# A graph layer with experts on one core: the order check's list and the x rows for u loaded behind z, u begun with the first edge tile

## The chip, the cores and the metric

The kernel runs on one core of a Trainium2 chip. Times are microseconds of device time of one execution, and smaller is better. The core has five engines with a queue of instructions each: TensorE (PE, with its weight loads shown as PEld), VectorE (DVE), ScalarE (ACT), GpSimd (POOL) and SyncE (SP). An engine takes its queue in order and waits on semaphores that other engines and transfers raise. SP, ACT and POOL also issue the transfers (DMA).

## What is computed

`x` has 6250 rows of 256 numbers, and there are 100000 edges `src -> dst`, sorted by `dst`. A graph layer is followed by a layer of 8 experts of which each row uses two:

```python
h = layernorm(x)
msg_sum = segment_sum(h[src], dst);  deg = segment_sum(1, dst)
agg = msg_sum / maximum(deg, 1)
x = x + concat([h, agg]) @ W.T + b                     # W: 256 x 512
n = layernorm(layernorm(x)) * gamma + beta
w = softmax of the top 2 of (n @ Wr + br)              # 8 experts
x = x + sum_e w[e] * (gelu(n @ W1[e] + b1[e]) @ W2[e] + b2[e])
```

## The kernel before, in words

The product with W is split in two. Its right half is applied to every row before the edges are summed: `z = layernorm(x) @ W_right.T`, with eight more columns that hold the router's logits. Its left half gives `u = x + layernorm(x) @ W_left.T + b`, with the same eight columns. Both are written to memory as `z_d` and `u_d`. Then `x1 = u + (sum of z over a row's edges) / deg`.

**The z stage** (`z_block`, line 278) runs over 13 blocks of four 128-row tiles, the last block being one tile. For each tile TensorE forms `product(t, 1)` (line 260, two products of depth 128, into the tiles `ph` and `pm` in turn), ScalarE scales it by `rstd_x` into `zt` (284), and SP writes `z_d` (287). VectorE takes the statistics of x some tiles ahead (`ahead`, lines 184 and 185) and makes `rstd_x` of eight tiles at a time (173 to 179). After each pair of tiles from block 5 on, one piece of other work is taken from the list `steps`: constants, the placing of the windows, the check that `dst` is sorted (`check_order`, 310 and 311, which compares `dst` with the same list moved by one, `follow`), and the sum of all checks (`sum_wrongs`, 366). SP loads x and its transpose four blocks ahead; behind the first four blocks stand the loads of `dst_i`, `src_i`, `follow` (302 to 304) and `gb_sb`.

**Between z and the edges** the left half of W is made ready: its router columns (`router_columns(0)`, 226 and 228), the biases spread over lanes (233 and 234), the columns' mean taken off (`center_weights(0)`, 248 to 253), and the biases' products (`add_biases`, 241 to 243). 28 tiles `xg` that will hold gathered rows get a column of ones (485).

**The edge stage.** The edges are cut into 56 windows of 14 tiles of 128 edges, 784 edge tiles in all. For an edge tile POOL gathers 128 rows of `z_d` by `src_i` into one of the 28 `xg` tiles (`gather`, 566), VectorE has made a matrix of zeros and ones from `dst` (`hot_tiles`, 574 and 577, seven edge tiles at a time), and TensorE adds the product of the two to the window's sum `pS` (`add_edges`, 583, two passes). A gather for tile t + 28 may start once the edge tile t has been added. The loop over edge tiles is a list of ticks: at each tick one edge tile is added, one gather is issued, and functions that `at(tick, f)` put down for later are called. When a window ends, its sum is shared with the next window through memory (589, 593, 597, 605), `u_d` is fetched (610) and x1 is formed (623 to 625). Each four windows go through the routing (493 to 537, 541 to 551, 631 to 663), the sorting of rows (670, 673) and, from 60 ticks after their end, the experts (849, 854, 862, 866), whose instructions TensorE's queue holds between the edge tiles.

**The u stage** has no place of its own. `u_stages()` issues the x loads of three pairs of tiles and returns 26 steps. A step loads x for a pair three steps on (197), adds the bias row (376), forms two products (260) and adds them in (383, 384), and writes the pair before to `u_d` (388). Before the first edge tile six steps are taken; then one step at every second tick, so that the last comes at tick 38. Then the memory of the u stage is handed to the experts: `xe` is cleared in four parts (828, ticks 3, 8, 13 and 18 later) and 16 loads bring the experts' weights (971, every second tick).

All five engines are under a schedule written by hand: each engine's queue holds the instructions in the order in which the program names them.

Of the kernel before, what the change touches and what calls it, by code (L numbers as in the profile page):

```python
# [8 lines left out]
F32 = mybir.dt.float32  # L9
I32 = mybir.dt.int32  # L10
# [7 lines left out]
P = 128  # L18
EPS = 1e-5
C = 14  # L20
# [7 lines left out]
XG = 28  # L28
# [2 lines left out]
@with_exitstack  # L31
def gnn_ffn_kernel(ctx: ExitStack, tc: tile.TileContext, x, x_cols, src, dst, dst_next, gw, gw_t, gb, gb_cols, gamma, beta,
                   wr, br, w1, b1, w2, b2, out):

# [32 lines left out]
    nc = tc.nc  # L67
# [6 lines left out]
    W = src.shape[1]  # L74
    DZ = D + NX
    DA = DZ + 1
# [22 lines left out]
    const = ctx.enter_context(tc.tile_pool(name="const", bufs=1))  # L99
# [25 lines left out]
    edges = fast_pools.enter_context(tc.tile_pool(name="edges", bufs=1))  # L125
    rstd_x = edges.tile([P, NT], F32, name="rstd_x")
    u_pools = fast_pools.enter_context(ExitStack())
    u_pool = u_pools.enter_context(tc.tile_pool(name="u", bufs=2))
# [3 lines left out]
    early = early_pools.enter_context(tc.tile_pool(name="early", bufs=2, side="right"))  # L132
# [25 lines left out]
    lanei = early.tile([P, 1], I32, name="lanei", bufs=1)  # L158
    nc.gpsimd.iota(lanei, pattern=[[1, 1]], base=0, channel_multiplier=1)

    def constants():
        nc.vector.tensor_scalar(before, ej, 0.0, None, op0=ALU.is_lt)
        nc.scalar.activation(cols, coli, AF.Copy)
        nc.vector.tensor_copy(lane, lanei)
        nc.vector.tensor_scalar(upper, col, lane, None, op0=ALU.is_gt)
# [79 lines left out]
    def center_weights(h):  # L245
        pc = ps.tile([P, DZ], F32, name="pm")
        for k in range(KD):
            nc.tensor.matmul(pc, ones, gw_sb[:, h * KD + k, :], start=(k == 0), stop=(k == KD - 1))
        for k in range(KD):
            nc.vector.scalar_tensor_tensor(gc[:, h * KD + k, :DZ], pc, -1.0 / D, gw_sb[:, h * KD + k, :],  # L250
                                           op0=ALU.mult, op1=ALU.add)
            if h == 0:
                nc.vector.tensor_copy(gc[:, k, DZ:], rc[:, k, :])
# [36 lines left out]
            if between:  # L290
                between.pop(0)()

    src_i = const.tile([P, W, C], I32, name="src_i")
    dst_i = const.tile([P, W, C], I32, name="dst_i")
    wrong = const.tile([P, 3], F32, name="wrong")

    def load_edges():

        follow = early.tile([P, W, C], I32, name="follow", bufs=1)
        nc.sync.dma_start(dst_i, dst)
        nc.sync.dma_start(src_i, src)
        nc.sync.dma_start(follow, dst_next)
        return follow

    def check_order(follow, i):
        some = slice(i * W // 2, (i + 1) * W // 2)
        down = early.tile([P, W // 2, C], F32, name="down", bufs=1)
        nc.vector.tensor_tensor(down, dst_i[:, some], follow[:, some], op=ALU.is_gt)  # L310
        nc.vector.reduce_max(wrong[:, i:i + 1], down.rearrange("p g c -> p (g c)"), axis=AX.X)

# [56 lines left out]
    def u_stages():  # L369

        def load(B):
            B.x = load_x(u_pool, "xu", B.first, B.n, UB, 4)

        def one(B):
            B.ut = u_pool.tile([P, UB, DZ], F32, name="u_t", bufs=3)
            nc.vector.tensor_tensor(B.ut[:, :B.n, :D], B.x[:, :B.n, :],
                                    gb_sb[:, None, :].to_broadcast([P, B.n, D]), op=ALU.add)

        def two(B):
            for i in range(B.n):  # L380
                t = B.first + i
                pu = product(t, 0)
                nc.vector.tensor_tensor(B.ut[:, i, D:], pu[:, DZ:], gb_r, op=ALU.add)
                nc.vector.scalar_tensor_tensor(B.ut[:, i, :], pu[:, :DZ], rstd_x[:, t:t + 1], B.ut[:, i, :],  # L384
                                               op0=ALU.mult, op1=ALU.add)

        def put(B):
            nc.sync.dma_start(rows_of(u_d, B.first, B.n), B.ut[:, :B.n, :])

        pairs = []  # L390
        for t0 in range(0, NT, UB):
            B = Group()
            B.first, B.n = t0, min(UB, NT - t0)
            pairs.append(B)

        for B in pairs[:3]:
            load(B)
# [19 lines left out]

    for t0 in blocks[:4]:
        load_block(t0)
    follow = load_edges()  # L420
    gb_sb = u_pool.tile([P, D], F32, name="gb_sb", bufs=1)
    nc.sync.dma_start(gb_sb, bass.AP(tensor=gb.tensor, offset=gb.offset, ap=[[0, P], [1, D]]))
    placed_rows = []
    steps = [constants, lambda: placed_rows.append(place_windows()), lambda: check_order(follow, 0),
             lambda: spread_windows(placed_rows[0]), lambda: check_order(follow, 1), place_rows, check_windows,
             lambda: None, sum_wrongs]
    router_weights()
    router_columns(1)
    center_weights(1)
    ahead, t0 = [], 0  # L430
# [12 lines left out]
    for t0 in blocks:  # L443
        if t0 + 4 * TB in blocks:
            load_block(t0 + 4 * TB)
        elif t0 == blocks[-3]:
            u_tasks = u_stages()
        z_block(t0, steps if t0 >= blocks[5] else None)
    assert not ahead
    assert not steps  # L450
    router_columns(0)
    wide_b = router_biases()
    center_weights(0)
    add_biases(wide_b)
    zero = u_pool.tile([CAP, D], F32, name="zero", bufs=1)
    nc.vector.memset(zero, 0.0)
    early_pools.close()
# [15 lines left out]
    def weights(pool):  # L473
# [5 lines left out]
        for e in range(0, NX, 2):  # L479
            parts += first[e + 2:e + 4] + second[e:e + 2]  # L480
        return w1_sb, w2_sb, parts

    xg = [edges.tile([P, DA], F32, name=f"xg{i}") for i in range(XG)]
    for g in xg:
        nc.vector.memset(g[:, DZ:], 1.0)


    def variances(G):
# [80 lines left out]

    def hot_tiles(V, c):  # L570

# [398 lines left out]
    def at(t, f, *args):  # L970
        later.setdefault(max(t, now), []).append(lambda: f(*args))
# [85 lines left out]
    def new_window(g, V_before):  # L1057
        V = Group()
        V.g, V.before, V.hot = g, V_before, []
        hot_tiles(V, 0)  # L1060
        return V

    V = new_window(0, None)
    edge_tiles = [(g, c) for g in range(W) for c in range(C)]
    for g, c in edge_tiles[:XG]:
        gather(g, c)
    for _ in range(6):
        u_tasks.pop(0)()
    for index in range(W // CW):
        K = Group()  # L1070
        K.index, K.first = index, index * CW
# [193 lines left out]
```

## Time and profile before

| | |
|---|---|
| median of 5 runs | 1445.03 us (1436.97 to 1447.31) |
| profiled execution | 1435.43 us, its span 1433.6 us |
| busy in the span | PE 1106.7, POOL 844.2, DVE 698.4, ACT 452.9 us |
| mean granted clock of TensorE | 0.886 of full speed |
| last z_d write issued, first gather | 64.35 and 67.78 us |
| first edge tile on TensorE | 79.84 us |
| last u product on TensorE | 161.26 us |

Engine names with a q at the end (SPq, POOLq) are what that engine's queue issues. In a line of the timeline the columns are start, duration, engine, line of the kernel, operation, tiles written and read, shape, count, and in brackets the idle time of the engine before it and what ended that. An edge tile is two records of line 583, a u or z product four records of line 260 (each product is two matmuls of two passes). The profiled execution lies 9.6 us below the median of the runs.

### The profile page before, as it was taken

How to read it: one execution, taken by the hardware profiler on the slowest of the kernel's cores; microseconds unless marked ns; L12 is line 12 of the kernel's file. 1: busy time of each engine (PE TensorE's matmuls, PEld its weight loads, DVE VectorE, ACT ScalarE, POOL GpSimd, SP SyncE). 2: the span in 40 equal slices, each digit the busy share in tenths (PEclk: the TensorE clock that was granted, in tenths of full speed). 3: DMA queues.
4: the chain of work that ended last, by engine and by line, in shares of the span. 5: the costliest groups of instructions: out<-in, count | busy, mean ns of one | idle time of the engine just before them, and what ended most of it. 6: DMA issues, size and time to landing. Idle time of an engine off the chain costs nothing.

```text
span 1433.6 us, 19064 instructions
## 1 busy us (share of the span) xinstructions
PE 1106.7 (77%) x5236; PEld 908.4 (63%) x5236; DVE 698.4 (49%) x2426; ACT 452.9 (32%) x1264; POOL 844.2 (59%) x892
## 2 busy tenths in 40 slices
PE   7858736696987969788786969798798887967752
PEld 6737524575866757576675758567687765855641
DVE  5736745362544545355453625465452544565323
ACT  2300002332342433334242324434323433435210
POOL 0076666666656666666566666666666666554552
PEclk9979978798987979999898989999999998988866
DMA  9878894545445454545445454554545454565543
GB/s 340 308 230 255 258 311 118 114 125 126 126 123 124 123 122 128 130 114 138 119 128 114 133 128 120 122 137 120 129 125 135 121 132 118 139 177 150 151 145 119
DMA packets 151610, 217.67 MB, mean 152 GB/s; under 512 B 37587, under 2 KB 119158, under 8 KB 151370
## 3 DMA queue, kind: packets, MB, share of 16 engines
q0 software_dynamic: 42768, 118.97, 33.3%
q1 hardware_dynamic: 100394, 87.97, 19.3%
q10 hardware_dynamic: 8336, 9.45, 2.0%
q8 instruction: 44, 0.72, 0.2%
q14 instruction: 68, 0.56, 0.1%
HBM read 163.97 MB, written 52.32 MB: 151 GB/s over the span
## 4 chain that ended last, share of the span: by engine, by line
PE 51%; issue 17%; DVE 10%; ACT 7%; another core or an unknown queue 6%; DMA 4%; ACTq 2%; SPq 2%; POOL 1%; POOLq 0%; DVEq 0%
PE pS L583 18%; PE ph L849 14%; PE py L862 10%; PE pm L670 4%; ACT xe L824 3%; PE py L910 2%; PE ph L892 2%; ACT hid L854 1%; ACTq L813 1%; DVE hot L577 1%; PE ph L260 1%; DMA xg<-y_d,plans 1%; PE pm L260 1%; DMA u_d<-u_t 1%
## 5 line engine op out<-in xcount | busy, mean ns | idle before, releaser
L566 POOL DMA_INDIRECT xg<-z_d,src_i x784 | 747.1, 953 | 476.7 <-issue 178.2
L583 PE MATMUL pS<-xg,hot 128*128 128x265 f32 x1568 | 446.6, 418 | 68.1 <-issue 55.6
L583 PEld LDWEIGHTS pS<-xg,hot 128*128 128x128 f32 x1568 | 312.6, 207 | 138.2 <-issue 72.9
L849 PE MATMUL ph<-xe,w_sb 128*128 128x128 f32 x1792 | 268.7, 298 | 94.9 <-issue 87.3
L849 PEld LDWEIGHTS ph<-xe,w_sb 128*128 128x128 f32 x1792 | 250.3, 210 | 118.9 <-issue 100.8
L862 PE MATMUL py<-w_sb,hid 128*128 128x256 f32 x896 | 229.1, 398 | 43.3 <-issue 19.6
L862 PEld LDWEIGHTS py<-w_sb,hid 128*128 128x128 f32 x896 | 176.3, 200 | 83.0 <-issue 48.4
L854 ACT ACTIVATE hid<-ph,b_sb 128x128 f32<-128x128 f32 x448 | 126.3, 375 | 295.4 <-remote 157.6
L824 ACT ACTIVATE xe<-xs x448 | 139.5, 311 | 90.6 <-issue 47.8
L577 DVE TENSOR_TENSOR hot<-cols,rel 128x896 f32<-128x896 f32 x112 | 121.2, 1082 | 87.1 <-PE pS L583 53.0
L941 POOL DMA_INDIRECT xg<-y_d,plans x98 | 95.0, 969 | 100.7 <-DMA out_dram<-xg 41.2
L866 DVE TENSOR_TENSOR rows<-py,b_sb 128x512 f32<-128x512 f32 x56 | 38.3, 685 | 155.0 <-PE py L862 37.7
L589 DVE TENSOR_TENSOR pS<-pS,row 1x265 f32<-1x265 f32 x55 | 23.5, 426 | 183.3 <-PE pS L583 84.9
L593 ACT ACTIVATE sums<-pS 128x265 f32<-128x265 f32 x56 | 22.0, 392 | 251.0 <-issue 101.5
L673 ACT ACTIVATE xs<-pm,beta_sb,gamma_sb 128x256 f32<-128x256 f32 x112 | 57.3, 568 | 135.6 <-PE pS L583 57.1
L260 PE MATMUL ph<-gc,x_t 128*128 128x264 f32 (+1 forms) x200 | 58.6, 418 | 19.8 <-remote 9.0
L670 PE MATMUL pm<-to,xn 128*128 128x256 f32 x224 | 59.9, 387 | 14.1 <-DVE to L663 4.2
L625 DVE SCALAR_TENSOR_TENSOR x<-pS,rdeg,x 128x264 f32<-128x264 f32 x55 | 27.1, 493 | 72.8 <-DMA x<-u_d 48.7
L260 PE MATMUL pm<-gc,x_t 128*128 128x264 f32 (+1 forms) x192 | 55.3, 413 | 8.4 <-DVE u_t L384 6.3
L260 PEld LDWEIGHTS ph<-gc,x_t 128*128 128x128 f32 x200 | 38.6, 201 | 32.5 <-remote 10.5
L670 PEld LDWEIGHTS pm<-to,xn 128*128 128x128 f32 x224 | 41.2, 190 | 26.5 <-issue 8.3
L948 DVE SCALAR_TENSOR_TENSOR xg<-xg,plans,xg 128x256 f32<-128x256 f32 (+1 forms) x98 | 46.0, 483 | 23.9 <-DMA xg<-y_d,plans 15.2
(196 smaller groups left out, 821.0 us busy)
## 6 DMA issues: line engine op xcount, KB each, us to landing
y_d<-rows SPq DMA_DIRECT2D x56, 256.0 KB
xg<-z_d,src_i POOLq DMA_INDIRECT x784
w_sb<-w_dram ACTq DMA_DIRECT2D x16, 512.0 KB
sums_d<-sums SPq DMA_DIRECT2D x55, 132.5 KB
x<-u_d SPq DMA_DIRECT2D x55, 132.0 KB
x_d<-x SPq DMA_DIRECT2D x55, 128.0 KB
u_d<-u_t SPq DMA_DIRECT2D x24, 264.0 KB
x_t<-x_cols_dram SPq DMA_DIRECT2D x12, 512.0 KB
```

What stands on the lines that cost most here:

```text
L260: nc.tensor.matmul(pz, x_t[:, t, k, :], gc[:, h * KD + k, :n], start=(k == 0), stop=(k == KD - 1))
L566: nc.gpsimd.indirect_dma_start(out=xg[(g * C + c) % XG][:, :DZ], out_offset=None, in_=z_d[:, :], in_offset=bass.IndirectOffsetOnAxis(ap=sr ...
L577: nc.vector.tensor_tensor(hot, col[:, None, :].to_broadcast([P, HC, P]), V.rel[:, c:c + HC, None].to_broadcast([P, HC, P]), op=ALU.is_equal)
L583: nc.tensor.matmul(V.pS, V.hot[c // HC][:, c % HC, :], xg[(V.g * C + c) % XG], start=(c == 0), stop=(c == C - 1))
L670: nc.tensor.matmul(px[:, k, :], G.xn[i][:, k * P:(k + 1) * P], G.one_hot[i], start=True, stop=True)
L673: nc.scalar.activation(xs[:, at:at + 2 * P], px[:, k, :], AF.Identity, bias=beta_sb[:, k:k + 1], scale=gamma_sb[:, k:k + 1])
L824: nc.scalar.activation(xe[:, :, bass.ds(to_at, CAP)], src[:, :, bass.ds(src_at, CAP)], AF.Copy)
L849: nc.tensor.matmul(ph[:, i, a * SH:(a + 1) * SH], w1_sb[:, U.e + a, k, c * P:(c + 1) * P], xe[:, k, at:at + SH], start=(k == 0), stop=(k = ...
L854: nc.scalar.activation(U.hid[:, c, a * SH:(a + 1) * SH], ph[:, i, a * SH:(a + 1) * SH], AF.Gelu, bias=b1_sb[:, U.e + a, c:c + 1])
L862: nc.tensor.matmul(U.py[:, h, :], U.hid[:, c, h * P:(h + 1) * P], w2_sb[:, U.e + h, c, :], start=(c == 0), stop=(c == KH - 1))
L941: nc.gpsimd.indirect_dma_start(out=V.y2[r], out_offset=None, in_=y_d[:K.batch.end_row, :], in_offset=bass.IndirectOffsetOnAxis(ap=plans[:c ...
L948: nc.vector.scalar_tensor_tensor(V.o, V.y2[r], plans.bitcast(F32)[:count, n, 2 + r:3 + r], V.o, op0=ALU.mult, op1=ALU.add)
```

## The change

- `follow` is no longer loaded behind the first four blocks but behind the whole of z and behind the first three x loads of u; its tile and that of `check_order` move into the memory of u. `check_order` and `sum_wrongs` leave the list `steps` and are called at the ticks 6, 12 and 18 of the edge loop.
- The first three x loads of u, which were issued ahead of the last three blocks of z, are issued behind z.
- `router_columns(0)`, `router_biases()`, `center_weights(0)` and `add_biases()` become pieces of `steps`, between the products of z.
- The ones of the 28 `xg` tiles are written in the piece `constants`.
- The six u steps before the first edge tile are gone. The 26 steps come at the even ticks 0 to 50.

```diff
     def constants():
+        for g in xg:
+            nc.vector.memset(g[:, DZ:], 1.0)
...
     def load_edges():
-        follow = early.tile([P, W, C], I32, name="follow", bufs=1)
         nc.sync.dma_start(dst_i, dst)
         nc.sync.dma_start(src_i, src)
+    def load_follow():
+        follow = u_pool.tile([P, W, C], I32, name="follow", bufs=1)
         nc.sync.dma_start(follow, dst_next)
         return follow
...
-    steps = [constants, lambda: placed_rows.append(place_windows()), lambda: check_order(follow, 0),
-             lambda: spread_windows(placed_rows[0]), lambda: check_order(follow, 1), place_rows, check_windows,
-             lambda: None, sum_wrongs]
+    steps = [constants, lambda: placed_rows.append(place_windows()), lambda: router_columns(0),
+             lambda: spread_windows(placed_rows[0]), lambda: wide_b.append(router_biases()),
+             lambda: center_weights(0), place_rows, lambda: add_biases(wide_b[0]), check_windows]
...
     for t0 in blocks:
         if t0 + 4 * TB in blocks:
             load_block(t0 + 4 * TB)
-        elif t0 == blocks[-3]:
-            u_tasks = u_stages()
         z_block(t0, steps if t0 >= blocks[5] else None)
-    router_columns(0)
-    wide_b = router_biases()
-    center_weights(0)
-    add_biases(wide_b)
+    u_tasks = u_stages()
+    follow = load_follow()
...
-    xg = [edges.tile([P, DA], F32, name=f"xg{i}") for i in range(XG)]
-    for g in xg:
-        nc.vector.memset(g[:, DZ:], 1.0)
...
     for g, c in edge_tiles[:XG]:
         gather(g, c)
-    for _ in range(6):
-        u_tasks.pop(0)()
+    at(6, check_order, follow, 0)
+    at(12, check_order, follow, 1)
+    at(18, sum_wrongs)
```

More of the change, by code (lines that the diff above doesn't have):

```diff
@@ L159, in gnn_ffn_kernel @@
     nc.gpsimd.iota(lanei, pattern=[[1, 1]], base=0, channel_multiplier=1)
+    src_i = const.tile([P, W, C], I32, name="src_i")
+    dst_i = const.tile([P, W, C], I32, name="dst_i")
+    xg = [edges.tile([P, DA], F32, name=f"xg{i}") for i in range(XG)]
     def constants():
+        for g in xg:
+            nc.vector.memset(g[:, DZ:], 1.0)
         nc.vector.tensor_scalar(before, ej, 0.0, None, op0=ALU.is_lt)
@@ L291, in z_block @@
                 between.pop(0)()
-    src_i = const.tile([P, W, C], I32, name="src_i")
-    dst_i = const.tile([P, W, C], I32, name="dst_i")
     wrong = const.tile([P, 3], F32, name="wrong")
     def load_edges():
-        follow = early.tile([P, W, C], I32, name="follow", bufs=1)
         nc.sync.dma_start(dst_i, dst)
         nc.sync.dma_start(src_i, src)
+    def load_follow():
+        follow = u_pool.tile([P, W, C], I32, name="follow", bufs=1)
         nc.sync.dma_start(follow, dst_next)
@@ L308, in check_order @@
         some = slice(i * W // 2, (i + 1) * W // 2)
-        down = early.tile([P, W // 2, C], F32, name="down", bufs=1)
+        down = u_pool.tile([P, W // 2, C], F32, name="down", bufs=1)
         nc.vector.tensor_tensor(down, dst_i[:, some], follow[:, some], op=ALU.is_gt)
@@ L419, in gnn_ffn_kernel @@
         load_block(t0)
-    follow = load_edges()
+    load_edges()
     gb_sb = u_pool.tile([P, D], F32, name="gb_sb", bufs=1)
@@ L423, in gnn_ffn_kernel @@
     placed_rows = []
-    steps = [constants, lambda: placed_rows.append(place_windows()), lambda: check_order(follow, 0),
-             lambda: spread_windows(placed_rows[0]), lambda: check_order(follow, 1), place_rows, check_windows,
-             lambda: None, sum_wrongs]
+    wide_b = []
+    steps = [constants, lambda: placed_rows.append(place_windows()), lambda: router_columns(0),
+             lambda: spread_windows(placed_rows[0]), lambda: wide_b.append(router_biases()),
+             lambda: center_weights(0), place_rows, lambda: add_biases(wide_b[0]), check_windows]
     router_weights()
@@ L1061, in new_window @@
         return V
+    now = 0
     V = new_window(0, None)
```

## The prediction

> **What bounds the kernel now.** I read the table of stages first, then the chain of waits, then the timeline of the first edge tiles. The table (engines' busy time, granted clock, DMA share, GB/s in each stretch):
>
> ```profile
> 11.00:63.40 52.40, 47.31 (x200) 38.52 (x201) 38.85 (x177) 22.25 (x57) 0.00 (x0) 1.00 1.04 365
> 63.40:67.80 4.40, 4.04 (x27) 3.66 (x26) 2.25 (x38) 0.48 (x1) 0.02 (x1) 1.00 0.62 199
> 67.80:79.60 11.80, 10.25 (x44) 7.79 (x43) 9.89 (x38) 0.00 (x0) 9.06 (x10) 1.00 0.75 227
> 79.60:109.00 29.40, 13.58 (x36) 8.66 (x35) 6.26 (x16) 0.00 (x0) 19.48 (x21) 0.62 0.67 207
> 109.00:162.10 53.10, 46.48 (x190) 37.06 (x189) 36.07 (x97) 0.79 (x2) 35.03 (x35) 0.95 0.86 262
> 180.60:215.50 34.90, 10.15 (x37) 7.46 (x36) 16.28 (x43) 2.50 (x5) 22.69 (x24) 0.72 0.89 303
> 256.00:1433.00 1177.00, 930.92 (x4555) 771.26 (x4553) 551.33 (x1898) 411.85 (x1159) 716.86 (x754) 0.89 0.49 129
> ```
>
> The columns are PE, PEld, DVE, ACT, POOL. From 256 us TensorE carries the kernel, and the change touches nothing there: what is won or lost before comes out at the end one for one. The z stage moves 365 GB/s with its DMA engines full. The odd row is 79.6 to 109: PE, DVE and DMA are all half idle, while POOL issues gathers one behind the other. The timeline shows what stands still:
>
> ```profile
> 86.25 0.17 DVE L383 TENSOR_TENSOR u_t<-ph,gb_r 128x8 f32<-128x8 f32 x1 [3.66 <-remote]
> 87.09 2.15 PE L260 MATMUL ph<-gc,x_t 128*128 128x272 f32 x4 [2.90 <-remote]
> ...
> 98.93 0.17 DVE L383 TENSOR_TENSOR u_t<-ph,gb_r 128x8 f32<-128x8 f32 x1 [6.14 <-remote]
> ...
> 103.92 0.95 POOL L566 DMA_INDIRECT xg<-z_d,src_i  x1 [0.30 <-issue]
> 106.63 0.17 DVE L383 TENSOR_TENSOR u_t<-pm,gb_r 128x8 f32<-128x8 f32 x1 [7.01 <-issue]
> ...
> 107.47 2.15 PE L260 MATMUL pm<-gc,x_t 128*128 128x272 f32 x4 [5.55 <-DVE u_t L384]
> ...
> 109.00 0.94 POOL L566 DMA_INDIRECT xg<-z_d,src_i  x1 [4.13 <-remote]
> ```
>
> Line 383 waits for u products whose matmuls the trace shows long done (the one read at 98.93 began at 80.29). TensorE's results reach the others one at a time: those of products 9, 10, 11, 12 and 13 at 81.30, 86.25, 90.50, 98.93 and 106.63, 6.3 us apart. POOL has run without a break since 67.78; its last free tile is filled by the gather at 103.92, and 2.7 us behind that all is normal. The same is seen far from here, in the experts (764 us on: POOL resumes after a pause, eight gathers later TensorE crawls, and recovers when POOL has to wait again):
>
> ```profile
> 764.12 0.94 POOL L566 DMA_INDIRECT xg<-z_d,src_i  x1 [2.60 <-remote]
> ...
> 772.65 0.27 PE L849 MATMUL ph<-xe,w_sb 128*128 128x128 f32 x1 [0.37 <-issue]
> ...
> 774.08 0.27 PE L849 MATMUL ph<-xe,w_sb 128*128 128x128 f32 x1 [1.16 <-issue]
> ...
> 775.48 0.27 PE L849 MATMUL ph<-xe,w_sb 128*128 128x128 f32 x1 [1.13 <-issue]
> ...
> 778.67 0.94 POOL L566 DMA_INDIRECT xg<-z_d,src_i  x1 [2.37 <-remote]
> ```
>
> So I take it that an unbroken run of some eight gathers slows TensorE until POOL pauses. That is inferred from coincidence, not shown.
>
> **The change part by part.** The sum is against the profiled execution, 1435.43 us (span 1433.6); the median of the runs is 9.6 higher, and I carry the difference over to it.
>
> *z stage.* TensorE gains the pieces that stood at 63.4 to 66.7: router columns 0.95, centring 1.13, biases 0.51 + 0.59, and loses 0.19 of `sum_wrongs`: +3.0 us. Its idle time there is 52.4 - 47.3 = 5.1 us, 1.76 of it at 49.7 behind the `rstd_x` of tiles 32 to 39, so between none and all of the 3.0 is hidden. VectorE gains 0.40 (28 ones), 0.17, 0.28 + 0.29, 2 x 0.43 + 2 x 0.16, 0.16 + 0.16 = 2.64 and loses 2 x (0.53 + 0.56) + 0.12 = 2.30: +0.34. The loads moved out are 0.40 MB (`follow`) and 0.79 MB (three pairs of x); at 365 GB/s 1.1 and 2.2 us. Ends: -3.3 to +3.0. I take 0, near their middle: where z ends, TensorE runs without a gap at 0.89 us a product, which lets neither end through whole.
>
> *Start of the gathers.* The first, at 67.78, waits for the last z write (issued 64.35). That write remains, so 67.8 stays, plus what z gives. The ones of `xg` on VectorE ended at 67.75; they move, and as the gather writes other columns I take the write for what it awaited. SP has three x loads and `follow` (0.4 to 0.7 us each to issue, 2.7 in all) between the last z write and the load of u's first tick; u's first x lands 2.67 behind its issue (the row at 65.11), about 68, before it is read. Cost 0; if POOL's start slips with z, everything slips with it.
>
> *TensorE between z and the first edge tile.* Before, products 0 to 9 of u (0.91 us each) ran from 66.7 to 77.2 under the first gathers. Now the first edge tile stands ahead of them and needs its gather: a gather lands 3 to 4 us behind its issue (3.45 and 3.68 in the chain), so TensorE idles from about 65 to 70.8. That cover is gone, and the ten products come later: 9.1 us of TensorE.
>
> *The slow stretch.* From 70.8 a pair of one edge tile (0.45) and one product (0.91) takes 1.36 us, so five pairs are done by 77.5, where the slow stretch began in this trace, ten gathers into the run. In it a pair takes the 6.3 us of above. POOL now stops when gather 28 + (edge tiles done) has no tile: 67.8 + 1.25 x (28 + 5 + (t - 77.5)/6.3) = t gives 117, with 11 pairs done, and 2.7 us later, at 120, the stretch is over. Before, it was over at 107 to 109 with 17 products done.
>
> *The rest of u.* Product 17 began at 107.47 and product 48 at 161.26: 1.735 us for one product and one edge tile. Products 12 to 48: 37 x 1.735 = 64.2, so u is through at 184 instead of 162.2. Then seven edge tiles instead of nineteen are left of the first four windows, at the 0.95 of that stretch (18.0 us for 19): 190.9 against 180.2. **+10.7 us.** Ends: with the stretch over at 109 and nine products done, 109 + 39 x 1.735 + 6.6 = 183.3, +3; with the POOL run one slot cycle longer (126), +17.
>
> *VectorE in u.* `check_order` at ticks 6 and 12 (1.09 each) and `sum_wrongs` (0.12) add 2.3 us; behind them on VectorE stand `hot` and line 376, and TensorE awaits those. Their list lands before tick 6, so they wait for nothing. Between 0 and 2.3; I take 0, since VectorE is busy 36.07 of 53.1 us in the stretch that such ticks resemble (109 to 162.1).
>
> *Ticks 38 to 50.* The clears of `xe` (2.17 each) move 12 ticks; of the four, the last two now fall among the routing of the first four windows, which TensorE awaits at 215.5. 0 to +4.3; I take 0, as two clears stood in that chain before and were followed by waits on transfers (5.35 us at 187.84). The weights (16 loads) shift likewise; they are needed at tick 116.
>
> Sum: 0 + 10.7 = 10.7; 1435.4 + 10.7 = 1446.1 profiled, **1455.7** against the median; I say 1455.
>
> One rule speaks against the change too. The row: the granted clock was 0.62 in 79.6 to 109, and a product took 2.15 us at 87.09 instead of 1.08. The Trainium skill, "TensorE: Matmul & The Clock Gate", Part 1, says that an idle window of some 3.4 us halves TensorE's clock and that as much activity restores it. By it the idle from 65 to 70.8 would put the first 3.4 us of edge tiles at half speed, an estimate of 1.7 us more; the sum above leaves that out.
>
> **The rivals.**
> - *A, faster: the slow stretch does not come.* It stood between products that ran ahead and 28 gathers; if it is not POOL's run that makes it, or if pauses below eight gathers break it, u runs at 1.735 from the start: 70.8 + 49 x 1.735 + 6.6 = 162.4 against 180.2, -17.8, **1427**. For it: between 110 and 118 POOL issued seven gathers in a row without harm. Against it: the first 28 gathers have free tiles in either kernel. It decides if POOL's first unbroken run ends before some 12 gathers.
> - *B, no change: the loss is taken up behind u.* In 180.6 to 215.5 TensorE is busy 10.15 of 34.9 us. If what it awaits there hangs on transfers and not on the end of the fourth window, 10 us vanish: **1445**, 4 either way. Against it: the routing starts from that window's x1.
> - *C: the z stage gets longer,* by up to the 3.0 of TensorE's pieces, +3 behind whichever of the others holds; it is in the range.
>
> **How the numbers follow.** The slow stretch recurring, 0.52 (1448 to 1462 with its own ends); A 0.28; B 0.20. Half a per cent is 7.2 us, about what a measurement of this kernel can tell from no change. Of the forecast four fifths are beyond 7.2 (0.42), the rest within; nearly all of A is faster (0.26); of B three fifths lie within, a fifth on each side. Slower 0.46, same 0.26, faster 0.28. The range takes in A's centre and the upper end of the slow stretch with z's 3.0 and the clears' 4.3: 1427 to 1466.
>
> **What the profile after would show.** Right: first gather near 67.8; first edge tile near 71, with TensorE idle before it; a stretch from about 78 in which line 383 waits for products long done, ending where POOL first waits for a tile, near 117; the last u product near 183; the fourth window's end near 191. Wrong: no such stretch with POOL still unbroken (then my cause is wrong, and A holds); or the stretch, but the first experts no later than before (B); or the last z write later than 66 (C).

## The result, and the profile after

The changed kernel takes 1443.93 us (median of 36 runs, 1432.58 to 1451.14), the kernel before 1441.95 (62 runs, 1432.56 to 1450.82). The ratio is 1.0012, with a 95% interval of 0.9999 to 1.0024: +1.7 us, between -0.1 and +3.5. The forecast of 1455 us is not what happened, and its case B, "no change", is where the time came out. The profiled execution of the changed kernel took 1446.93 us, its span 1445.1.

The engines' busy time by stage, in the stretches in which the prediction showed them (columns PE, PEld, DVE, ACT, POOL, the granted clock, the share of the DMA, GB/s), kernel after:

```profile
11.00:63.40 52.40, 49.17 (x208) 40.94 (x209) 38.81 (x210) 21.74 (x55) 0.00 (x0) 0.97 0.98 343
63.40:67.80 4.40, 2.43 (x11) 1.72 (x10) 0.00 (x0) 1.71 (x4) 0.00 (x0) 1.00 0.50 171
67.80:79.60 11.80, 3.88 (x9) 3.01 (x10) 3.91 (x19) 0.00 (x0) 8.06 (x9) 0.62 0.95 322
79.60:109.00 29.40, 12.42 (x47) 9.32 (x45) 4.30 (x12) 0.00 (x0) 22.40 (x24) 0.73 0.54 152
109.00:162.10 53.10, 43.43 (x168) 33.38 (x169) 34.90 (x93) 0.79 (x2) 31.80 (x33) 0.88 0.78 225
180.60:215.50 34.90, 17.14 (x56) 12.75 (x56) 23.33 (x48) 2.50 (x5) 24.88 (x27) 0.78 0.94 306
256.00:1433.00 1177.00, 932.25 (x4558) 778.92 (x4558) 552.03 (x1897) 413.32 (x1166) 717.38 (x757) 0.88 0.50 129
```

From 67.8 to 79.6 TensorE has lost its cover (3.88 us busy instead of 10.25), as forecast. From 79.6 to 109 it is as slow as before (12.42 instead of 13.58). From 180.6 to 215.5 it does 7 us more than before (17.14 instead of 10.15): the last u product and edge tiles of the first windows, which before stood earlier, now fall there. The next lines are the timeline of the start and of the slow stretch, kernel after:

```profile
75.72 1.22 PE L580 MATMUL pS<-xg,hot 128*128 128x265 f32 x2 [9.90 <-DMA xg<-z_d,src_i]
76.74 2.02 PE L267 MATMUL ph<-gc,x_t 128*128 128x272 f32 x4
...
81.52 1.08 PE L267 MATMUL ph<-gc,x_t 128*128 128x272 f32 x4
...
84.25 1.08 PE L267 MATMUL ph<-gc,x_t 128*128 128x272 f32 x4
...
86.10 0.17 DVE L387 TENSOR_TENSOR u_t<-pm,gb_r 128x8 f32<-128x8 f32 x1 [2.77 <-issue]
...
98.69 0.17 DVE L387 TENSOR_TENSOR u_t<-ph,gb_r 128x8 f32<-128x8 f32 x1 [11.30 <-remote]
...
108.49 0.17 DVE L387 TENSOR_TENSOR u_t<-pm,gb_r 128x8 f32<-128x8 f32 x1 [9.11 <-remote]
...
109.75 0.94 POOL L563 DMA_INDIRECT xg<-z_d,src_i  x1 [0.30 <-issue]
115.02 0.94 POOL L563 DMA_INDIRECT xg<-z_d,src_i  x1 [4.33 <-remote]
...
116.95 0.17 DVE L387 TENSOR_TENSOR u_t<-ph,gb_r 128x8 f32<-128x8 f32 x1 [7.17 <-remote]
...
118.16 0.56 DVE L314 TENSOR_TENSOR down<-dst_i,follow 128x392 f32<-128x392 int32 x1
```

The slow stretch came back, with the same features: the reads of u products wait 7 to 11 us for products that TensorE had begun long before (the one read at 98.69 began at 84.25), and it is over at 117, just behind POOL's first longer pause (idle for 4.33 us up to the gather at 115.02). The prediction had POOL stop at 117 and the stretch over at 120.

A few moments of single profiles on chips where the kernel before takes some 1440 to 1455 us, in us. A window's end is the end of its last edge tile on TensorE (the prediction's 180.2 for the fourth is 179.7 so read); "sorting" is the first product that sorts rows for experts (line 670 of the kernel before). A third value of before is from the kernel that holds TensorE in window 30 (below), which is the same up to there.

| moment | before | after |
|---|---|---|
| last scaling of z | 63.8, 64.3, 64.5 | 65.9 |
| first gather | 67.8, 68.9, 68.5 | 69.1 |
| first edge tile | 79.8, 79.7, 79.2 | 75.7 |
| last u product's end | 162.3, 163.5, 163.1 | 181.7 |
| fourth window's end | 179.7, 179.9, 179.4 | 184.9 |
| first sorting | 222.1, 224.4, 224.2 | 228.0 |
| 224th edge tile | 426.2, 427.8, 424.8 | 428.6 |
| 784th edge tile | 1255.7, 1259.5 | 1259.4 |
| span | 1433.6, 1442.0 | 1445.1 |

u ends 19 us later, the fourth window 5, the last edge tile 0 to 4. The two spans of the unchanged kernel differ by 8.4 us, half of it behind the last edge tile (177.9 and 182.5 us): a single pair of spans says nothing of a change of this size.

### The profile page after: what moved, and what is told of

Read it like the earlier page. It is cut to its first block, busy times and chain, and to the rows that moved or that the text cites. A ratio compares the mean times of both kernels' runs of the same rounds, so it can differ in the third digit from the quotient of the medians.

```text
span 1445.1 us, 19054 instructions
## 1 busy us (share of the span) xinstructions
PE 1107.7 (77%) x5236; PEld 916.9 (63%) x5236; DVE 698.0 (48%) x2426; ACT 452.8 (31%) x1264; POOL 843.7 (58%) x892
## 4 chain that ended last, share of the span: by engine, by line
PE 56%; issue 18%; DVE 9%; ACT 5%; DMA 4%; another core or an unknown queue 4%; SPq 2%; ACTq 1%; POOL 1%; POOLq 0%; DVEq 0%
PE pS L580 19%; PE ph L846 16%; PE py L859 11%; PE pm L667 3%; ACT xe L821 2%; PE ph L889 2%; PE py L907 2%; DMA u_d<-u_t 1%; DVE hot L574 1%; PE ph L267 1%; ACT hid L851 1%; ACTq L810 1%; PE pm L267 1%; DVE st L191 1%
## 5 line engine op out<-in xcount | busy, mean ns | idle before, releaser
L580 PEld LDWEIGHTS pS<-xg,hot 128*128 128x128 f32 x1568 | 312.0, 206 | 141.2 <-issue 80.4
L846 PE MATMUL ph<-xe,w_sb 128*128 128x128 f32 x1792 | 272.1, 302 | 112.9 <-issue 94.4
L846 PEld LDWEIGHTS ph<-xe,w_sb 128*128 128x128 f32 x1792 | 254.0, 214 | 138.8 <-issue 110.7
L851 ACT ACT_TABLE_LOAD x24 | 30.8, 1283 | 71.5 <-PE pS L580 54.7
```

The costliest lines, as they stand in the source:

```text
L580: nc.tensor.matmul(V.pS, V.hot[c // HC][:, c % HC, :], xg[(V.g * C + c) % XG], start=(c == 0), stop=(c == C - 1))
L846: nc.tensor.matmul(ph[:, i, a * SH:(a + 1) * SH], w1_sb[:, U.e + a, k, c * P:(c + 1) * P], xe[:, k, at:at + SH], start=(k == 0), stop=(k = ...
L851: nc.scalar.activation(U.hid[:, c, a * SH:(a + 1) * SH], ph[:, i, a * SH:(a + 1) * SH], AF.Gelu, bias=b1_sb[:, U.e + a, c:c + 1])
```

## Experiments

The study fell on chips of two kinds: on three the kernel before took medians of 1441.75, 1454.94 and 1443.66 us, on two 1209.81 and 1211.66. Each chip was used on one occasion, so what belongs to the chip and what to the occasion is not told apart. Each comparison of times below is with runs of before on the same chip; the moments of profiles are mostly compared across chips.

### The kernel before once more

No edit; for a second profile.

> The kernel before once more, unchanged, for a second profile of it. It tells how far two profiles of one kernel differ at the same places. If single profiles are good to about 1 us up to the fourth window's end (179.7 us) and to the first sorting (222.1), then the +5.2 and +5.9 us that the changed kernel's profile shows there are the change's. If they scatter by 5 us or more, those readings are worth nothing. The tail behind the last edge tile (177.9 us in the profile of before, 185.7 in that of after) is expected to scatter by several us.

Its profile is in the table: up to the fourth window the two agree to 0.5 us except for the start of the gathers and the end of u (1.1 each), at the first sorting they differ by 2.3. So the 5 us at the fourth window are the change's; of the later ones half could be chance.

### u begun with the first edge tile, alone; and the rest of the change, alone

```diff
-    for _ in range(6):
-        u_tasks.pop(0)()
```

> The kernel before with the six u steps ahead of the first edge tile left out, so that u begins with the first edge tile; nothing else is changed. The theory of the prediction (u late by 22 us, the fourth window late by 10.7, and that carried to the end): about +8 to +11 us. Rival 1 (the fourth window is late by only some 3 us, since edge tiles get ahead in the slow stretch when no u products stand before them, and that is carried to the end): +2 to +4. Rival 2 (the loss is taken up behind u): between -1 and +1, with the fourth window's end still late in the profile.

0.9993 (0.9975 to 1.0011), -1.0 us, with the fourth window's end at 185.1 and the first sorting at 226.4. The other way round, in the kernel after:

```diff
+    for _ in range(6):
+        u_tasks.pop(0)()
     at(6, check_order, follow, 0)
```

> The changed kernel with the six u steps put back ahead of the first edge tile; the rest of the change stays. The theory of the prediction: 8 to 11 us less than the changed kernel, so 6 to 9 less than before. Rival 1: 2 to 4 us less than the changed kernel, the z stage's 2 us remaining. Rival 2: as the changed kernel within 1 us.

1.0008 (0.9989 to 1.0027), +1.2 us; the fourth window ends at 184.0, the first sorting is at 226.5. So, against the mean of 179.7 in before, u's late start by itself costs 5.4 us at the fourth window, the rest of the change, with its late z (last scaling at 68.3 in this profile, first gather at 71.5), 4.3, and both together 5.2: in these single profiles they do not add. At the end none of the three is told from before. The theory of the prediction, 8 to 11 us, is out; with the time unchanged and the fourth window late, the first kernel does what its Rival 2 said.

Where the lateness of u goes is seen on TensorE behind u. First the kernel before, then the kernel after (line 583 of before and 580 of after are the edge tiles):

```profile
162.18 2.40 PE L583 MATMUL pS<-xg,hot 128*128 128x265 f32 x10
167.17 3.37 PE L583 MATMUL pS<-xg,hot 128*128 128x265 f32 x14 [2.59 <-issue]
174.57 5.08 PE L583 MATMUL pS<-xg,hot 128*128 128x265 f32 x14 [4.04 <-issue]
```

```profile
179.04 1.06 PE L580 MATMUL pS<-xg,hot 128*128 128x265 f32 x4
180.57 1.16 PE L267 MATMUL ph<-gc,x_t 128*128 128x272 f32 x4 [0.47 <-issue]
181.56 3.29 PE L580 MATMUL pS<-xg,hot 128*128 128x265 f32 x14
186.93 0.46 PE L580 MATMUL pS<-xg,hot 128*128 128x265 f32 x1 [2.08 <-issue]
```

With u done, the kernel before adds edge tiles in lots of seven and waits 2.59 and 4.04 us in between. In the kernel after there are u products at that time, which fill these waits, and the last tiles of the window then run at 0.45 us each without one.

### A hold on TensorE of known length

The first edge tile of window 3 (the fourth) or of window 30 is formed 44 times more, and overwritten:

```diff
     def add_edges(V, c):
...
+        for _ in range(44 if V.g == 3 and c == 0 else 0):
+            nc.tensor.matmul(V.pS, V.hot[0][:, 0, :], xg[V.g * C % XG], start=True, stop=True)
...
```

> The kernel before with TensorE held for about 20 us at the first edge tile of the fourth window: that tile's product is formed 44 times more (about 0.45 us each) and overwritten. The theory of the prediction (what the fourth window loses comes out at the end one for one): the fourth window ends near 200 instead of 180, the first sorting near 242 instead of 222, and the time is 20 us longer. Theory that the loss is taken up behind u: the fourth window near 200, the sorting between 222 and 242, the 224th edge tile (426 to 428) less than 5 us later, and the time less than 5 us longer.

> The same hold of about 20 us on TensorE, but at the first edge tile of window 31, in the middle of the experts. If TensorE's work bounds the time from 256 us on, as the prediction said, about +20 us. If POOL's gathers bound it, less than +10, since 28 gathered tiles (some 35 us of POOL's work) are ready ahead. It tells whether a loss at this place is carried where one at the fourth window is not.

The holds and what stands behind the first, kernel with the hold in the fourth window:

```profile
168.22 21.58 PE L584 MATMUL pS<-xg,hot 128*128 128x265 f32 x88 [3.94 <-issue]
189.64 12.67 PE L585 MATMUL pS<-xg,hot 128*128 128x265 f32 x56
...
239.90 1.10 PE L672 MATMUL pm<-to,xn 128*128 128x256 f32 x4 [3.68 <-DVE to L665]
```

21.6 us held; the fourth window ends at 196.1, the first sorting is at 239.9 and the 224th edge tile at 441.3. Against the profile of the same chip (the third values of the table) that is +17, +16 and +17: some 5 us of the hold were taken up within the fourth window, whose tiles then run without a wait (second line). The time is 1.0139 (1.0119 to 1.0158), +20 us with 17 to 23. In window 30, 19.8 us held are 1.0131 (1.0089 to 1.0174), +19 with 13 to 25. So a loss of this size at the fourth window is carried to the end: for it that sentence of the prediction holds, and the routing behind it, rival B's place, takes up no more than 1 us. That a loss of 5 us is carried too does not follow. A hold stops POOL at once, and the late u does not: the 71st gather is at 190.5 with the hold, at 173.2 in the kernel after and at 170.0 and 171.5 in before. But at the 106th gather the kernel after is 4.3 us behind the mean of these two profiles of before, so POOL does fall behind there too, only later.

### Fewer gathered tiles for the first four windows

```diff
+RING, RT = 8, 56
...
+    def slot(t):
+        return t % RING if t < RT else t % XG
...
-            out=xg[(g * C + c) % XG][:, :DZ], out_offset=None, in_=z_d[:, :],
+            out=xg[slot(g * C + c)][:, :DZ], out_offset=None, in_=z_d[:, :],
...
```

The loop over the edge tiles, not shown, issues the gathers as these tiles come free, at most two at a tick.

> The kernel before with the first 56 edge tiles gathered into 8 tiles instead of 28, so that POOL has to wait for an edge tile after its first eight gathers; from then on 28 as before. Theory that POOL's unbroken run makes the slow stretch: no waits of over 2 us on finished u products between 80 and 117 us, products and edge tiles at 1.7 us a pair from 80 us on, u through near 144 instead of 162, the fourth window's end near 162 instead of 180, and up to 18 us less at the end if that is carried. Theory that something else makes it (the u products' own transfers, the clock): the slow stretch stays, the fourth window ends at 180 or later, and the time is the same or longer.

1.0025 (1.0001 to 1.0048): slower by 3.6 us. But the profile says something else than the time (stages as above, then moments of the timeline):

```profile
79.60:109.00 29.40, 27.89 (x120) 22.00 (x118) 19.53 (x52) 0.39 (x1) 18.36 (x19) 1.00 0.97 314
...
180.00:212.00 32.00, 3.01 (x10) 1.65 (x10) 1.75 (x5) 0.06 (x1) 21.02 (x22) 0.58 0.45 121
```

```profile
205.48 0.95 POOL L570 DMA_INDIRECT xg<-z_d,src_i  x1 [0.30 <-issue]
207.76 0.94 POOL L570 DMA_INDIRECT xg<-z_d,src_i  x1 [1.33 <-remote]
212.42 0.43 DVE L593 TENSOR_TENSOR pS<-pS,row 1x265 f32<-1x265 f32 x1 [28.27 <-remote]
212.66 0.94 POOL L570 DMA_INDIRECT xg<-z_d,src_i  x1 [3.96 <-remote]
...
215.76 0.66 PE L647 MATMUL pm<-both,ones 128*128 128x64 f32 x2 [30.68 <-issue]
```

The slow stretch is gone: TensorE is busy 27.89 of 29.4 us instead of 13.58, u is through at 138.6, the fourth window at 162.6 instead of 179.7. Then the ring opens to 28 tiles, POOL issues 43 gathers in a row from 152.7 to 205.5, and TensorE and VectorE all but stand still from 184 on, until POOL pauses. The first sorting is at 224.3, as in before. The gain was taken by a second, worse slow stretch that the edit itself made.

### The data or the issuing

For the first four windows 88 numbers a row are gathered instead of 264, from other rows of z (the sums of these windows are not the reference's). The tiles are cleared on POOL first.

```diff
     for g in xg:
         nc.vector.memset(g[:, DZ:], 1.0)
+        nc.gpsimd.memset(g[:, :DZ], 0.0)
...
-            out=xg[(g * C + c) % XG][:, :DZ], out_offset=None, in_=z_d[:, :],
+            out=xg[(g * C + c) % XG][:, :DZ // 3 if g < 4 else DZ], out_offset=None,
+            in_=z_d.rearrange("r (a c) -> (r a) c", a=3) if g < 4 else z_d[:, :],
```

> The kernel before with gathers of 88 numbers a row instead of 264 for the first four windows (from a view of z of three times as many rows, so that the rows are others and the sums of these windows are not the reference's); POOL issues as many gathers and descriptors. 28 clears of the tiles are added on POOL, which is idle then. If the data that the gathers move make the slow stretch, it is gone or much shorter, and u is through before 150. If POOL's issuing makes it, it stays: finished u products read some 6 us apart from 80 to 107, u through near 162.

This one fell on a chip on which before takes 1209.81 us, and where the changed kernel (profile below) has no slow stretch either: no answer. Again:

> The kernel with the narrow gathers (88 numbers a row instead of 264 in the first four windows, other rows, so that the sums of these windows are not the reference's) once more, since the chip of the first time shows no slow stretch in the unchanged kernel either. Where before takes some 1440 us: if the data make the slow stretch, it is gone or much shorter and u is through before 150; if POOL's issuing makes it, finished u products are read some 6 us apart from 80 to 107 and u is through near 162.

On a chip with 1443.66 us for before, the timeline of VectorE and POOL:

```profile
89.48 0.17 DVE L383 TENSOR_TENSOR u_t<-pm,gb_r 128x8 f32<-128x8 f32 x1 [4.24 <-remote]
107.68 0.17 DVE L383 TENSOR_TENSOR u_t<-ph,gb_r 128x8 f32<-128x8 f32 x1 [16.91 <-remote]
108.61 0.95 POOL L567 DMA_INDIRECT xg<-z_d,src_i  x1 [0.30 <-issue]
113.29 0.17 DVE L383 TENSOR_TENSOR u_t<-pm,gb_r 128x8 f32<-128x8 f32 x1 [4.92 <-remote]
114.24 1.16 POOL L567 DMA_INDIRECT xg<-z_d,src_i  x1 [4.68 <-remote]
```

With a third of the data the stretch is as long (until 113; the product read at 107.68 began at 83.35), and u ends at 161.4. It is not the amount of data; it goes with the run of gathers that POOL issues. Each of them still fetches 128 rows, so the issuing and the number of transfers are not told apart.

### Fewer gathered tiles throughout

```diff
+RING = 8
...
-            out=xg[(g * C + c) % XG][:, :DZ], out_offset=None, in_=z_d[:, :],
+            out=xg[(g * C + c) % RING][:, :DZ], out_offset=None, in_=z_d[:, :],
...
-                if t + XG < len(edge_tiles):
-                    gather(*edge_tiles[t + XG])
+                if t + RING < len(edge_tiles):
+                    gather(*edge_tiles[t + RING])
```

In these two kernels the last gathers of results take tiles that are overwritten before they are added, so part of the output is not the reference's, and less of that work runs side by side: their ends are not to be read.

> The kernel before with all edge tiles gathered into 8 tiles in place of 28, so that POOL never issues more than about eight gathers in a row; the other 20 tiles are left to the last gathers of the experts' results. Theory that long unbroken runs of POOL make the slow stretches: none is left (no products of the experts 0.7 us apart for more than 3 us, against 14 such stretches of some 130 us together in the profile of before), the u stage is through near 140 as with 8 tiles in its first part, no standstill at 180 to 212. If TensorE then goes on at its own pace, up to 40 us less at the end. Against it: POOL loses the room to run ahead, and where TensorE works 10 us on experts, gathers stop: up to 40 us more. Theory that the stretches have another cause: they remain.

> As the last one, with 12 tiles in place of 28. By the theory of the unbroken run: slow stretches remain, but short (a run of at most 12 gathers, from the eighth on, 5 us each), the time between before and the kernel with 8, or less than both if 8 tiles are too few to run ahead. By the theory of another cause: slow stretches as before.

8 tiles: 1.0040 (1.0019 to 1.0061); 12 tiles: 0.9976 (0.9947 to 1.0006). Between 79.6 and 109 TensorE is busy 27.40 and 24.03 us, u ends at 141.2 and 145.0, the first sorting is at 198.5 and 202.6 (224.2 with 28 tiles on this chip), the 224th edge tile at 410.5 and 408.6 (424.8), the 672nd at 1085.1 and 1083.7. From there to the end they take 378.0 and 363.9 us. The two kernels with a hold, on the same chip and with the end of before, take 350.7 and 351.7, so the disturbed end costs 12 to 27 us and hides what was won. In the experts the stretches become fewer, not none: the times between neighbouring first products of an expert (line 849 of before) that start 0.6 to 3 us apart add up to 79 and 86 us, against 119 and 121 in the two profiles of before. The expectation "none is left" did not hold.

### Twelve tiles, then wider; in both kernels

```diff
+RING, WIDE = 12, 504
...
+    def slot(t):
+        return t % (RING if t < WIDE else XG)
...
+                if t > WIDE and t % 14 == 0:
+                    lead = min(lead + 1, XG)
+                while fetched < min(t + 1 + lead, len(edge_tiles)):
+                    gather(*edge_tiles[fetched])
+                    fetched += 1
```

> The kernel before with 12 gathered tiles instead of 28 up to edge tile 504; from then on the number grows by one with each window to 28, so that the end is that of before. Theory that POOL's unbroken run makes the slow stretch of 80 to 117 us, that the stretch costs some 20 us up to the first sorting (202.6 with 12 tiles throughout, 222 to 224 before), and that a shift at this place is carried to the end as the 22 us of the hold were: 15 to 22 us less than before. Theory that such a gain is given back in the experts, which lose room to run ahead: between -5 and +5.

> The changed kernel with the same 12 tiles up to edge tile 504. If the change's small loss comes from the slow stretch that its late u meets, it goes with it: the fourth window ends within 2 us of that of before with 12 tiles (some 161), and the times differ by under 3 us. If it comes from z, which ends 2 us later, and from the u products that lost their place under the first gathers, the changed kernel stays 3 to 8 us behind before with 12 tiles.

Both fell on the chip with 1209.81 us: 1.0088 (1.0065 to 1.0110) and 1.0059 (1.0039 to 1.0080). Without a slow stretch the short ring only costs. Again:

> The kernel before with 12 gathered tiles up to edge tile 504 once more, for a chip with the slow stretch. Where before takes some 1440 us: 15 to 22 us less than before if the stretch costs what the profiles with 8 and 12 tiles show up to the first sorting and a gain there is carried to the end; within 5 us of before if it is given back. Where before takes some 1210 us: 8 to 11 us more than before again, as the first time (1.0088).

> The changed kernel with 12 gathered tiles up to edge tile 504 once more. Where before takes some 1440 us: within 3 us of before with 12 tiles if the change's small loss hangs on the slow stretch, 3 to 8 us behind it if it comes from z and from the u products' lost place.

On the chip with 1443.66 us: 1.0008 (0.9987 to 1.0030) and 0.9993 (0.9967 to 1.0019). The 501st edge tile of the first is at 805.7, against 832.1 and 835.0 in before; at the 529th the lead is down to 6 to 9 (875.1 against 881.1 and 884.5). In between the tiles of the wider ring were free at once, and POOL issued 26 gathers in a row (timeline of the kernel from before, TensorE and POOL):

```profile
840.05 0.60 PE L587 MATMUL pS<-xg,hot 128*128 128x265 f32 x1 [1.52 <-issue]
847.59 1.26 PE L853 MATMUL ph<-xe,w_sb 128*128 128x128 f32 x4 [6.94 <-issue]
850.77 0.94 POOL L570 DMA_INDIRECT xg<-z_d,src_i  x1 [0.30 <-issue]
852.93 0.94 POOL L570 DMA_INDIRECT xg<-z_d,src_i  x1 [1.21 <-remote]
857.83 1.19 POOL L570 DMA_INDIRECT xg<-z_d,src_i  x1 [3.96 <-remote]
859.67 0.65 PE L587 MATMUL pS<-xg,hot 128*128 128x265 f32 x1
```

TensorE crawls from 825 to 857 and goes on when POOL pauses: the same picture as in the first windows, 700 us on. A lead of 20 to 30 us over the profiles of before had held for 600 us, from the first sorting at 197.1 on, so a gain there is carried too, until POOL gets another long run. In the changed kernel POOL issues 33 gathers in a row there (814.9 to 854.9), and its lead over the kernel after, 24 us at the 501st edge tile, is gone at the 529th.

### The changed kernel once more, on a chip without the stretch

> The changed kernel once more, unchanged, for a second profile. Last scaling of z near 66 if z is longer for good (65.9 in the first profile, 63.2 to 64.7 in eight profiles of kernels with the z stage of before), near 64 if that was chance; the fourth window's end near 185 and the first sorting between 226 and 228 if these are the change's.

It fell on the chip with 1209.81 us for before and took 1209.25 in its one run. Stages of its profile:

```profile
79.60:109.00 29.40, 28.76 (x125) 23.41 (x124) 21.82 (x57) 0.39 (x1) 22.40 (x24) 0.98 0.89 260
256.00:1205.00 949.00, 845.45 (x4360) 701.20 (x4358) 528.82 (x1833) 397.96 (x1120) 700.46 (x736) 0.93 0.62 156
```

POOL issues its first 40 gathers in a row (68.8 to 118.7), later 645 in a row, and TensorE is busy 28.76 of 29.4 us. The last scaling of z is at 65.6: z is longer in this profile too. On this chip u ends at 152.6 and the fourth window at 155.7.

### Twelve and sixteen tiles to the end

As "throughout", with the tiles for the last gathers taken in an order that leaves them all 28.

> The kernel before with 12 gathered tiles for all 784 edge tiles; the tiles for the last gathers of results are taken in an order that leaves them 28, as before. In the kernel that widened from 12 to 28 tiles, the 501st edge tile was 26 to 29 us earlier than in before, and then POOL issued 26 gathers in a row (819 to 851) while two thirds of a window stood still, which took 22 us back. Theory that a gain at the first sorting is carried to the end unless POOL gets another unbroken run: 20 to 30 us less than before, where before takes some 1440 us. Theory that the experts lose what the shorter ring wins: within 8 us of before. Where before takes some 1210 us: up to 11 us more.

> The changed kernel with 12 gathered tiles for all edge tiles. Without the slow stretch the u products' late start has no price by the theory that the stretch makes it, and z's later end has one of 2 to 4 us: 0 to 5 us more than before with 12 tiles, so 16 to 30 less than before where that takes some 1440 us. By the prediction's sum for a u without slow stretch (162.4 against 180.2 for the fourth window) the changed kernel would be even with or ahead of it.

> The kernel before with 16 gathered tiles for all edge tiles. If a run of more than about ten gathers is what slows TensorE, the first run of 16 makes a short slow stretch (from 78 to about 90) and the later ones some, so between 12 tiles and before: 10 to 25 us less than before where that takes some 1440 us. If only much longer runs do harm, as with 12 tiles.

They fell on the chip with 1211.66 us: 1.0151 (1.0121 to 1.0180), 1.0125 (1.0097 to 1.0153) and 1.0101 (1.0073 to 1.0130). So they do not show what these rings do to the slow stretch. The changed kernel is not behind before on the chips without the stretch: its median with the full ring of 12 is 1226.09, that of before with it 1230.32; with the widened ring they are 1218.78 and 1221.11. What a short ring to the end is worth on the other chips, with the end undisturbed, was not measured, and no version was shown to beat both kernels.

## Why the prediction was wrong, point by point

- **The base, 1445.03 us.** It is the median of 5 runs; 62 runs give 1441.95. Of the 11.8 us between the sum's 1455.7 and the measured 1443.93, 3.1 lie here and 8.7 in the change's +10.7.
- **z stage, taken as 0.** Wrong by its size, inside its ends. The last scaling is at 65.1 to 68.4 in six profiles of kernels with the new z stage, at 63.2 to 65.5 in fourteen with the old one: +2.3 in the means (66.5 and 64.3). The first gather follows by +1.0 only. Rival C was there, but in the profiles it does not add to the rest.
- **First edge tile near 71.** It came at 75.7, and TensorE idled 9.9 us, not 5.8. The gather of the first tile took 6.6 us from issue to use; in the kernel that only begins u later it took 3.7 (69.15 to 72.89). The moved loads of x and `follow`, issued from 66.8 to 68.8, are the likely reason: the DMA engines' busy share is 1.01 from 69 to 75.7 in the kernel after, and 0.78 from 69 to 73 in the other. No run has them alone; they were costed at 0. At the fourth window's end nothing is seen of it (184.9 and 185.1).
- **The clock rule, left out of the sum.** The row: the products at 76.74 and 78.55 took 2.02 us, the one at 81.52 1.08, and the granted clock of 67.8 to 79.6 is 0.62: behind the idle time TensorE ran at about half speed. The first edge tile, two products and two more edge tiles took 5.8 us (75.72 to 81.52) instead of 3.2 at 0.45 and 0.91 each, so 2.6 more, where the prediction estimated 1.7. The Trainium skill, "TensorE: Matmul & The Clock Gate", Part 1, says that an idle window of some 3.4 us halves the clock until TensorE has been busy for about as long. The trace agrees with the halving behind 9.9 us of idle time. What these 2.6 us cost behind the slow stretch no run tells apart.
- **The slow stretch recurs, ending near 117 to 120, with 11 pairs done.** It does, and is over at 116.95 with 11 edge tiles and 10 products formed. That the numbers agree is in part luck: POOL stopped at 110.7, 33 gathers in, where the sum had 117 and 39; the results came some 9 us apart (98.69, 108.49, 116.95), not 6.3; and the first late read is at 86.10, where the sum let the stretch begin at 77.5. Its cause was given as inferred; the runs show that it goes with POOL's unbroken run (gone with 8 tiles, another one when the ring opened, the same with a third of the data). They also show that the run is not enough: on two chips there is none, with up to 645 and 658 gathers in a row.
- **The rest of u, 64.2 us, u through at 184.** Right within 2.3 us (181.7).
- **"Then seven edge tiles instead of nineteen are left [...] at the 0.95 of that stretch": the step that failed.** 0.95 was the mean of a stretch of 17.5 us in which TensorE waited 6.6 (2.59 and 4.04) and, behind the second wait, took 5.08 us for seven tiles instead of 3.37. It was used as a cost per tile. In the kernel after, u products stand where these waits were, and what was left took 3.2 us instead of 6.6. These 3.4 us and the 2.5 by which u was through earlier than the sum had it (181.7 instead of 184.2), less 0.5 in how the end of before is read, make up the 5.5 by which the fourth window is less late than forecast (5.2 us instead of 10.7), to 0.1. What u is late by (19 us) is covered down to 5 by the waits that stood behind u and by the twelve edge tiles that are now added among its products.
- **"What is won or lost before comes out at the end one for one."** The second step that failed, at least for a loss of this size. It held for a hold of 21.6 us (17 at the fourth window, +20 at the end). For the 5 us here the profiles give 4 at the first sorting (means of 227.2 in two kernels with the late u, 223.6 in three without), 1 at the 224th edge tile, 2 at the 784th, and the times +1.7 (-0.1 to 3.5). Two profiles of one kernel differ by up to 4 us at these places, and a neighbouring edge tile can read otherwise (against the first two profiles of before the 205th is 3.5 us late in the kernel after, the 233rd 11), so the 1 and the 2 are not to be leaned on. That at most 3.5 of the 5.2 us reach the end is shown by the times; where the rest goes stays open.
- **Rivals.** A was wrong where the result was taken: the stretch came. On the other chips it comes in neither kernel, so A's gain is not there either (1209.25 in one run, against 1209.81). B's outcome came, but some 5.5 of the 10.7 us were covered ahead of the fourth window's end, among its own edge tiles, and not behind it. For the rest B's mechanism is neither shown nor excluded.
- **Two sums of the prediction.** The chances of its cases make 0.30 for faster and 0.24 for the same, not 0.28 and 0.26; and the slow stretch's upper end with 3.0 and 4.3 is 1469 us, not 1466. Neither changes the outcome.
- **VectorE's checks and the clears of `xe` at 0.** Nothing contradicts it: `check_order` ran at 118.16 behind the stretch. No run was made on them alone.

## What to carry to other kernels

A mean time per tile that contains waits is no cost per tile: before it is multiplied, the stretch has to be split into work and waits, since work that arrives late fills the waits first. A hold of known length on one engine, put at one place, tells how much of a loss of that size reaches the end; it also stops the engines that feed on the held one, so a smaller or otherwise made loss need not follow it, as here. And an edit that lifts a limit on an engine that runs ahead should be looked at in the profile where the limit ends, because the time alone can show no change where a gain and a loss of 20 us stand side by side.

## What the hardware did that was not expected

- On three chips a long unbroken run of gathers from POOL slows or stops TensorE and VectorE until POOL pauses: from 86 to 117 us in the kernel after (33 gathers in a row, one of which took half a microsecond longer), with almost a standstill of 30 us in a run of 43, and a crawl of 32 us in a run of 26. The results that the waiting engines want are long started. On two other chips nothing of it is seen: on one the kernel after itself keeps TensorE busy for 28.76 of 29.4 us, on the other kernels with rings of 12 and 16 do so for 27.4 to 28.9 us and go on through up to 658 gathers in a row; and the kernel before takes 1210 us instead of 1442 to 1455. What the chips differ in, and by what way a run of gathers holds the other engines, stays open; pauses put into POOL's queue with the ring left at 28 tiles were not tried.
- On two of those three chips a ring of 8 or 12 tiles kept beyond the start brings the first sorting to 198.5, 202.6 and 197.1, against 222.1 to 224.4 in the profiles of before: the stretch at the start costs some 20 to 27 us up to there.
